# Which pair of heads is masked first, and which engine normalises x: two edits to a four-layer kernel of convolutions and windowed attention

## The chip, the cores and the metric

The kernel runs on one core of one Trainium2 chip. A core has TensorE for matrix products (PE in the profile, its weight loads PEld), VectorE (DVE), ScalarE (ACT) and GpSimd (POOL) for elementwise work, SyncE (SP) that issues transfers, and 16 DMA engines. Each of them works off its own queue of instructions in order, and they wait for each other by semaphores. TensorE writes its results into PSUM[...], from where VectorE and ScalarE read them; GpSimd works on SBUF. The metric is the device time of one execution in microseconds, the median of several runs.

## The reference, cut to what matters

Four layers, each of the form x = x + layer(groupnorm(x)), on x of 4 x 256 x 48 x 48 in float32. Layer 0 builds a 7x7 dilated filter for every pixel from a convolution and a softmax; layers 1 and 2 are 3x3 convolutions with binary and ternary weights. The change is in layer 3, linear attention over boxes of three sizes:

```python
q = sigmoid(einsum('bchw,oc->bohw', x, Wq))      # 8 heads of 32 channels
k = sigmoid(einsum('bchw,oc->bohw', x, Wk))
v = einsum('bchw,oc->bohw', x, Wv);  v = v / max(norm(v, axis=1), 1e-12)
Ik, Ikv = integral(k), integral(einsum('bfhw,bghw->bfghw', k, v))
for w in (1, 2, 4):                              # boxes of 48, 24, 12 pixels
    wk, wkv = box(Ik, 48 // w), box(Ikv, 48 // w)
    attn = einsum('bdhw,bdfhw->bfhw', q, wkv)
    outs.append(attn / (einsum('bdhw,bdhw->bhw', q, wk) + 1e-6))
out = x + einsum('bchw,oc->bohw', concatenate(outs), Wout) + bout
```

Before it, x is group-normalised: (x - m) / sqrt(var + eps), with 32 groups of 8 channels.

## The kernel before, in words

The kernel doesn't form the integrals of k times v. For every block of 8 rows of queries it computes scores k·q against tiles of 8 x 16 keys, multiplies them by 0/1 masks that say which keys lie in the query's box of each of the three sizes, and sums masked scores times v. Layers 0 to 2 run first, image by image, with work of the next image mixed in; the last part is layer 3's attention, over a stream of 720 tiles of scores: 4 images x 2 halves of the channels (4 heads each) x 6 blocks of query rows `rb`, and for each of these the tiles `(a, c)` of keys, `a` the block of 8 rows and `c` one of three columns of 16. A tile is near when its rows fall into the smallest box (`a` at most one block from `rb`: 384 tiles), else far. As far as they last, near and far tiles alternate; what is left follows, mostly near or far alone. The order of all work on each engine is the order of the program.

For a tile `n`, the loop does this:

- `scores` (line 1694 on): TensorE writes `s` for two pairs of heads, first pair, then second. Each pair takes two PSUM banks, and there are two such buffers (`ps_s`), so the first pair of tile n+1 can be written only when the first pair of tile n has been read by all, and so the second.
- `masked` (line 1712): the heart of the change. ScalarE's `copy` takes out the columns where the largest box covers every key of the tile, so that no mask is needed. VectorE's `widest` multiplies the strips beside them by the mask of the largest box, and its `middle` makes the scores of the middle box out of the banks (near tiles only). GpSimd multiplies ScalarE's copy by the mask of the smallest box (near) or the middle one (far). In 192 of the far tiles there is `copy` and `widest`, in the remaining 144 tiles, at the edge of the largest box, only `widest` over the whole tile.
- `sums`: TensorE multiplies the masked scores of tile n-2 by `vs` (LAG = 2), so it has these sums to do between the scores of one tile and those of the next.
- `advance`: one step of the jobs that run beside: the projections to q, k, v of the next image (`Projection`, line 287), box sums of k (`k_sums`), the norms, the final product with `Wout` (`finish`).

`Projection.load` (line 301) fetches 8 rows of x into `xr` and writes them normalised and reordered into `xn`, one instruction for each half of the channels. It takes the mean and the reciprocal deviation from `st3`, which `layer2` fills at its end. It runs for 30 groups of rows, two instructions each: 12 groups for image 0 while layers 0 to 2 of image 3 are still at work, and 6 for each of images 1 to 3, beside the first blocks of the image ahead of it.

The calls whose order is at stake, in `masked`:

```python
first, second = zip(ss, pairs)
copy(*first)
middle(*second)
copy(*second)
middle(*first)
widest(*first)
widest(*second)
```

Every engine's instruction is recorded by one helper, so the profile shows line 142 for almost all; groups are told apart by the names of the tiles: `s` scores, `sm` masked scores, `acc` sums, `proj_ps` projections, `xn` normalised x, `sg`, `kt`, `vt` what ScalarE takes out of the projections.

Of the kernel before, what the change touches and what calls it, by code (L numbers as in the profile page):

```python
# [15 lines left out]
AF = mybir.ActivationFunctionType  # L16
ALU = mybir.AluOpType
# [128 lines left out]
def conv_preact_kernel(  # L146
# [50 lines left out]
    st3 = const.tile([P, B, 2, NCT], F32, name="st3")  # L197


    pe, dve, act, pool, sync = (  # L200
        InOrder(tc, e) for e in (nc.tensor, nc.vector, nc.scalar, nc.gpsimd, nc.sync)
    )
# [69 lines left out]
    def take(what):  # L272
        while free[what] == 0:
            yield 1
        free[what] -= 1
# [11 lines left out]
    class Projection:  # L287
# [13 lines left out]
        def load(self, g, a, n):  # L301

            b = self.b
            yield from take("xr")
            if self.enough:
                free["xr"] += 1
                self.left.append(g)
                return
            xr = self.scr.tile([P, NCT, RB, W], F32, tag="xr", name="xr")
            sync.dma_start(  # L310
                out=xr,
                in_=x3_d[b][:, a * RB : (a + 1) * RB, :].rearrange(
                    "(ct p) r w -> p ct r w", p=P
                ),
            )
            yield FETCH
            yield from take("xn")
            xn = self.scr.tile([P, NCT, NKC, P], F32, tag="xn", name="xn")
            for ct in range(NCT):
                dve.tensor_scalar(  # L320
                    xn[:, ct].rearrange("p c (r x) -> p c r x", x=KC),
                    xr[:, ct].rearrange("p r (c x) -> p c r x", x=KC),
                    st3[:, b, 0, ct : ct + 1],
                    st3[:, b, 1, ct : ct + 1],
                    ALU.subtract,
                    ALU.mult,
                )
                yield 1
            free["xr"] += 1
            self.xn[g], self.uses[g] = xn, n  # L330
# [102 lines left out]
        def groups(self, groups):  # L433

            def load(n):
                a, names = groups[n]
                return self.load(n, a, sum(NKC if name == "v" else 1 for name in names))

            yield load(0)
            for n, (a, names) in enumerate(groups):
                if n + 1 < len(groups):
                    yield load(n + 1)
                for name in names:
                    if name == "v":
                        for c in range(NKC):
                            yield self.v(n, a, c)
                    else:
                        yield self.qk(n, a, name[0], int(name[1]))  # L450


    with (
# [766 lines left out]
        def layer2(b, stats):  # L1220
# [102 lines left out]
            late()  # L1323
            fill(1.5)
            m3, r3 = stats.end(fill)
            dve.tensor_copy(st3[:, b, 0, :], m3)
            dve.tensor_copy(st3[:, b, 1, :], r3)

        def prelude(b):
# [99 lines left out]
        with (  # L1429
# [30 lines left out]
            for b in range(B):  # L1460
                if b + 1 < B:
                    filler = conv0(b + 1, {})
                else:
                    ending.close()
                    wts3 = ctx.enter_context(tc.tile_pool(name="wts_qkv", bufs=1, side="right"))
                    filler = project_first()
                    masks = wts3.tile([P, NMASK], BF16, name="masks")
                    nc.gpsimd.dma_start(out=masks, in_=masks_in[:, 0:NMASK])
                stats = attend(b)
                for _ in side:  # L1470
                    fill(1.5)
                load_wl1(0)
                load_wl1(1)
                load_wl2(0)
                layer2(b, layer1(b, stats))
                if b + 2 < B:
                    prelude(b + 2)
                else:
                    fill_all()
# [3 lines left out]
    with (  # L1483
# [187 lines left out]
        def rows_seen(wi, a, rb):  # L1671

            h = HALVES[wi]
            return (
                max(0, a * RB - h + 1 - rb * RB),
                min(RB, a * RB + RB + h - rb * RB),
            )

        def cols_seen(wi, c):
            h = HALVES[wi]  # L1680
            return max(0, c * KC - h + (wi > 0)), min(W, c * KC + KC + h)

        class Block:
# [28 lines left out]
            def masked(self, a, c, ss):  # L1712

                rb = self.rb
                all0 = rows_seen(0, a, rb), cols_seen(0, c)
                (r0, r1), (c0, c1) = all0
                wis = [wi for wi in range(NW) if seen(wi, a, rb)]
                pairs = [
                    {
                        wi: smp.tile(  # L1720
                            [P, 2, RB, min(W, KC + 2 * HALVES[wi])],
                            F32,
                            tag=f"sm{wi}",
                            name=f"sm{wi}",
                        )
                        for wi in wis
                    }
                    for _ in ss
                ]

                def view(tiles, wi, rows, cols):
                    (y0, _), (x0, _) = rows_seen(wi, a, rb), cols_seen(wi, c)
                    return tiles[wi][
                        :, :, rows[0] - y0 : rows[1] - y0, cols[0] - x0 : cols[1] - x0
                    ]

                def times_mask(engine, wi, rows, cols, dst, src):
                    mr = rb * RB + rows[0] - (a * RB - HALVES[wi] + 1)
                    mc = cols[0] - (c * KC - MCOL0[wi])
                    nr, ncol = rows[1] - rows[0], cols[1] - cols[0]  # L1740
                    m = mask[wi][:, mr : mr + nr, mc : mc + ncol]
                    engine.tensor_mul(
                        dst, src, m.unsqueeze(1).to_broadcast([P, 2, nr, ncol])
                    )

                def of_banks(s, tiles, wi, rows, cols):
                    src = s[:, :, rows[0] - r0 : rows[1] - r0, cols[0] - c0 : cols[1] - c0]
                    times_mask(dve, wi, rows, cols, view(tiles, wi, rows, cols), src)

                f0, f1 = max(0, c * KC + KC - HALVES[0]), min(W, c * KC + HALVES[0] + 1)
                full = abs(a - rb) * RB + RB <= HALVES[0]

                many = seen(NW - 1, a, rb)

                def middle(s, tiles):
                    if full and many:
                        of_banks(s, tiles, 1, rows_seen(1, a, rb), cols_seen(1, c))

                def copy(s, tiles):
                    if full:
                        act.copy(
                            view(tiles, 0, (r0, r1), (f0, f1)), s[:, :, :, f0 - c0 : f1 - c0]
                        )

                def widest(s, tiles):
                    if not full:
                        of_banks(s, tiles, 0, *all0)
                        return  # L1770
                    for p0, p1 in ((c0, f0), (f1, c1)):
                        if p0 < p1:
                            of_banks(s, tiles, 0, (r0, r1), (p0, p1))

                first, second = zip(ss, pairs)
                copy(*first)
                middle(*second)
                copy(*second)  # L1780
                middle(*first)
                widest(*first)
                widest(*second)
                for tiles in pairs:

                    wi = NW - 1 if many else 1
                    if wi in wis:
                        rows, cols = rows_seen(wi, a, rb), cols_seen(wi, c)
                        src = view(tiles, 0, rows, cols)
                        times_mask(pool, wi, rows, cols, view(tiles, wi, rows, cols), src)  # L1790
                return [
                    {wi: view(t, wi, rows_seen(wi, a, rb), cols_seen(wi, c)) for wi in wis}
                    for t in pairs
                ]
# [28 lines left out]
        def seen(wi, a, rb):  # L1823
            r0, r1 = rows_seen(wi, a, rb)
            return r0 < r1
# [226 lines left out]
```

## Time and profile before

| | |
|---|---|
| time, median of 3 runs | 3783.98 us (3771.21 to 3786.39) |
| span of the profiled execution | 3775.4 us |
| TensorE busy, matrix products | 3264.8 us (86%), mean granted clock 0.952 |
| VectorE busy | 2487.2 us (66%), 5119 instructions |
| ScalarE busy | 1036.2 us (27%), 2025 instructions |
| GpSimd busy | 1518.1 us (40%) |
| first scores of layer 3 | 1430 us after the start |
| normalisation of x for q, k, v | 60 instructions on VectorE, 39.2 us |
| masks by VectorE from PSUM | 2592 instructions, 1135.8 us |
| copies by ScalarE from PSUM | 1152 instructions, 594.9 us |

In a row of groups, the columns are line, engine, operation, output and input tiles with their shape, the count; then busy time and the mean of one in ns; then the idle time of the engine just before these instructions, and what ended it. In the timeline, the columns are start, duration, engine, operation, shape and count of the merged instructions, and in brackets the idle time before and its releaser. In the list of waits they are who waited for whom, the total, how often, and the longest, in us. A row of windows gives the stretch, its length, and each engine's busy time with the number of its instructions.

### The profile page before, as it was taken

How to read it: one execution, taken by the hardware profiler on the slowest of the kernel's cores; microseconds unless marked ns; L12 is line 12 of the kernel's file. 1: busy time of each engine (PE TensorE's matmuls, PEld its weight loads, DVE VectorE, ACT ScalarE, POOL GpSimd, SP SyncE). 2: the span in 40 equal slices, each digit the busy share in tenths (PEclk: the TensorE clock that was granted, in tenths of full speed). 3: DMA queues.
4: the chain of work that ended last, by engine and by line, in shares of the span. 5: the costliest groups of instructions: out<-in, count | busy, mean ns of one | idle time of the engine just before them, and what ended most of it. 6: DMA issues, size and time to landing. Idle time of an engine off the chain costs nothing. (4 is left out here: it accounts for less than half of the span.)

```text
span 3775.4 us, 68847 instructions
## 1 busy us (share of the span) xinstructions
PE 3264.8 (86%) x26498; PEld 1879.4 (50%) x26498; DVE 2487.2 (66%) x5119; ACT 1036.2 (27%) x2025; POOL 1518.1 (40%) x2184
## 2 busy tenths in 40 slices
PE   3688898998996788988889889899899899989998
PEld 2467686786784564433334334344443344444443
DVE  7876587587583366777666567756577766556665
ACT  0012111111113322433222333332344332233331
POOL 0000120020020034778765486755365766344332
PEclk9798999999997899999999899999999999999999
DMA  7745323324324313345434243533223444101122
GB/s 250 238 135 170 100 104 116 109 95 125 109 75 124 102 70 108 125 136 159 125 103 131 90 136 122 164 97 108 78 95 123 139 116 116 47 31 53 41 60 60
DMA packets 373019, 423.04 MB, mean 112 GB/s; under 512 B 129076, under 2 KB 328532, under 8 KB 371540
## 3 DMA queue, kind: packets, MB, share of 16 engines
q1 hardware_dynamic: 371491, 416.32, 35.6%
q8 instruction: 211, 3.46, 0.4%
q0 software_dynamic: 144, 1.52, 0.2%
q14 instruction: 117, 0.95, 0.1%
q10 hardware_dynamic: 1056, 0.79, 0.1%
HBM read 288.79 MB, written 131.25 MB: 111 GB/s over the span
## 5 line engine op out<-in xcount | busy, mean ns | idle before, releaser
L142 DVE TENSOR_TENSOR sm<-s,masks 128x112 f32<-128x112 f32 (+10 forms) x2592 | 1135.8, 493 | 765.5 <-PE s L142 321.1
L142 POOL TENSOR_TENSOR sm<-sm,masks 128x432 f32<-128x432 f32 (+14 forms) x1152 | 853.3, 755 | 936.5 <-ACT sm L142 672.0
L142 PE MATMUL s<-qs,ks 32*128 32x320 f32 (+3 forms) x5760 | 832.5, 500 | 200.1 <-DVE sm L142 151.2
L142 ACT COPY sm<-s 128x528 f32<-128x528 f32 (+2 forms) x1152 | 594.9, 535 | 1470.7 <-PE s L142 1169.9
L142 PE MATMUL acc<-sm,vs 128*32 128x384 f32 (+18 forms) x13440 | 880.5, 385 | 16.1 <-POOL sm L142 15.8
L142 PEld LDWEIGHTS s<-qs,ks 32*128 32x128 f32 x5760 | 374.1, 185 | 604.7 <-DVE sm L142 232.8
L142 PE MATMUL cv<-vx,wt 128*128 128x288 f32 x2080 | 559.3, 425 | 90.7 <-DVE vx L142 49.1
L142 PEld LDWEIGHTS acc<-sm,vs 128*32 128x32 f32 x13440 | 355.2, 110 | 551.3 <-issue 348.6
L142 PEld LDWEIGHTS cv<-vx,wt 128*128 128x128 f32 x2080 | 402.4, 198 | 212.4 <-issue 53.6
L142 POOL MEMSET v<- 128x16 f32 (+1 forms) x120 | 18.6, 215 | 725.7 <-DVE vx L142 635.7
L142 PE MATMUL cv<-v,wl 128*128 128x384 f32 x1152 | 224.5, 354 | 24.4 <-DVE x L142 9.2
L142 PEld LDWEIGHTS cv<-v,wl 128*128 128x128 f32 x1152 | 214.8, 195 | 34.6 <-issue 16.1
L142 POOL TENSOR_TENSOR pt<-pt 128x144 f32<-128x144 f32 x336 | 187.4, 558 | 22.8 <-DVE pt L142 0.5
L142 POOL TENSOR_TENSOR v<-l2v,v 128x384 fp32r<-128x384 f32 x96 | 109.2, 1168 | 130.2 <-ACT v L142 121.4
L142 POOL TENSOR_TENSOR nhi<-nhi,nq 128x384 f32<-128x384 f32 x144 | 148.3, 1058 | 0.0
L142 PE MATMUL cv<-pad,wl 128*128 128x384 bf16 x864 | 143.1, 327 | 0.0
L142 PE MATMUL out_ps<-o,wout_sb 128*128 128x384 f32 x288 | 122.8, 509 | 9.4 <-DVE o L142 5.4
L142 PE MATMUL out_ps<-stage,wout_sb 128*128 128x384 f32 x288 | 117.3, 489 | 0.4 <-DVE stage L142 0.4
L142 PE MATMUL proj_ps<-wv_sb,xn 128*128 128x256 f32 x288 | 89.5, 438 | 32.3 <-ACT vt L142 19.1
L142 DVE TENSOR_TENSOR vx<-v 128x868 f32<-128x868 f32 x112 | 115.4, 1056 | 0.5
L142 PE MATMUL ap<-seen,xT 120*128 120x120 f32 (+3 forms) x832 | 113.5, 293 | 0.0
L142 PEld LDWEIGHTS <-wl 128*128 128x128 bf16 x864 | 83.8, 97 | 59.1 <-issue 0.4
(162 smaller groups left out, 2859.0 us busy)
## 6 DMA issues: line engine op xcount, KB each, us to landing
wt<-wt SPq DMA_DIRECT2D x48, 768.0 KB
kb_d<-pt SPq DMA_DIRECT2D x48, 576.0 KB
rc<-r_d SPq DMA_DIRECT2D x192, 144.0 KB
nhi<-kb_d SPq DMA_DIRECT2D x120, 192.0 KB
nlo<-kb_d SPq DMA_DIRECT2D x88, 192.0 KB
o_d<-stage SPq DMA_DIRECT2D x24, 576.0 KB
o<-o_d SPq DMA_DIRECT2D x24, 576.0 KB
wl<-wl_d SPq DMA_DIRECT2D x16, 768.0 KB
```

The source lines that it names most:

```text
L142: return lambda *args, **kwargs: self.tc.keep_in_program_order(op(*args, **kwargs))
```

## The change

Two edits in layer 3. In `masked`, VectorE's `middle` now takes the first pair of heads ahead of the second, after both copies have been issued. In `Projection.load`, the rows of x are normalised by ScalarE in one activation, scale * x + bias, in place of VectorE's (x - m) * r; for this `layer2` stores -m * r in place of m.

```diff
@@ Projection.load
             for ct in range(NCT):
-                dve.tensor_scalar(
+                act.activation(
                     xn[:, ct].rearrange("p c (r x) -> p c r x", x=KC),
                     xr[:, ct].rearrange("p r (c x) -> p c r x", x=KC),
-                    st3[:, b, 0, ct : ct + 1],
-                    st3[:, b, 1, ct : ct + 1],
-                    ALU.subtract,
-                    ALU.mult,
+                    AF.Identity,
+                    bias=st3[:, b, 0, ct : ct + 1],
+                    scale=st3[:, b, 1, ct : ct + 1],
                 )
                 yield 1
@@ layer2
             m3, r3 = stats.end(fill)
-            dve.tensor_copy(st3[:, b, 0, :], m3)
+            dve.scalar_tensor_tensor(st3[:, b, 0, :], m3, -1.0, r3, ALU.mult, ALU.mult)
             dve.tensor_copy(st3[:, b, 1, :], r3)
@@ masked
                 first, second = zip(ss, pairs)
                 copy(*first)
-                middle(*second)
                 copy(*second)
                 middle(*first)
+                middle(*second)
                 widest(*first)
                 widest(*second)
```

## The prediction

> **What bounds the kernel now.** I read the busy times first, then stretches of the run, then the waits of the stretch that the change is in, then its groups of instructions by shape, and last the order in time of two tiles of scores. The chain of waits explains only a few per cent of this span, so I don't use it. The stretches before and after the first scores:
>
> ```profile
> core 0: us, PE busy (x) PEld busy (x) DVE busy (x) ACT busy (x) POOL busy (x), PEclk, DMA share, GB/s
> 0.00:1431.00 1431.00, 1184.39 (x5842) 936.56 (x5842) 940.38 (x1831) 262.55 (x489) 153.90 (x298) 0.92 0.40 128
> 1431.00:3775.00 2344.00, 2080.36 (x20660) 942.85 (x20656) 1546.86 (x3288) 773.64 (x1536) 1364.18 (x1886) 0.97 0.34 103
> ```
>
> Layer 3's attention is the second row: 2344 us, of which TensorE (PE) is busy 2080 and idle 264. VectorE (DVE) is busy 66% of it, ScalarE (ACT) 33%. The waits there, what TensorE waits for first:
>
> ```profile
> PE s L142 <- DVE sm L142: 151.2, 243, 3.9
> PE proj_ps L142 <- ACT sg L142: 18.3, 14, 6.1
> PE acc L142 <- POOL sm L142: 15.8, 17, 3.3
> ...
> DVE sm L142 <- PE s L142: 321.1, 342, 9.2
> DVE sm L142 <- ACT sm L142: 266.9, 181, 5.5
> ```
>
> More than half of TensorE's idle time (151 of 264 us) is one wait: new scores (`s`) can't be written until VectorE has masked the old ones out of the same banks. And VectorE waits 321 us for scores. The two wait for each other in turn: a loop, in which nothing is hidden whenever TensorE has no sums left to do. The shapes that matter:
>
> ```profile
> L142 ACT COPY sm<-s 128x528 f32<-128x528 f32 x384 | 229.1, 615 | 489.0 <-PE s L142 382.4 <-DVE sm L142 79.6 <-POOL sm L142 21.6
> L142 DVE TENSOR_TENSOR sm<-s,masks 128x624 f32<-128x624 f32 x256 | 194.9, 802 | 98.3 <-PE s L142 94.2 <-ACT sm L142 3.2 <-POOL sm L142 0.8
> L142 DVE TENSOR_SCALAR xn<-xr,st 128x384 f32<-128x384 f32 x60 | 39.2, 665 | 31.4 <-PE proj_ps L142 27.3 <-DMA xr<-x_d 4.1
> ```
>
> The first row is `copy`, the second `middle` for tiles of the middle columns, the third the normalisation that moves. `copy` waits 79.6 us for VectorE: that is the second pair's copy waiting until `middle` of the second pair has read the same scores. One tile in time, its loop closed on TensorE:
>
> ```profile
> 3028.46 1.19 PE L142 MATMUL s<-qs,ks 32*128 32x320 f32 x8 [0.83 <-DVE sm L142]
> 3029.36 0.51 ACT L142 COPY sm<-s 128x400 f32<-128x400 f32 x1 [1.43 <-PE s L142]
> 3029.68 1.78 DVE L142 TENSOR_TENSOR sm<-s,masks 128x448 f32<-128x448 f32 x4 [0.99 <-PE s L142]
> 3030.40 0.51 ACT L142 COPY sm<-s 128x400 f32<-128x400 f32 x1 [0.53 <-DVE sm L142]
> 3031.30 1.03 PE L142 MATMUL s<-qs,ks 32*128 32x320 f32 x8 [1.04 <-DVE sm L142]
> ```
>
> ScalarE starts on the first pair at 3029.36, VectorE on the second pair at 3029.68, only 0.32 us later; at 3030.40 ScalarE turns to the second pair. They never read one pair together.
>
> **What the Trainium skill says.** "PSUM — Partial Sum Buffer", section "PSUM bank collisions raise a hardware error": two engines may not touch one bank and quadrant at once, two readers included, and the compiler's scheduler puts a dependency between them. The trace agrees: over all 384 tiles with a `middle`, where VectorE waited for a copy it started 32 ns after the copy's end, and the second copy began 34 to 90 ns after `middle` of its pair. The same page, "Engine vs sequencer instructions", calls the queues of ScalarE and VectorE strict FIFO: what waits holds up what is behind it. "ScalarE: Activation LUTs", "Table sets: the hidden batching unit", puts cheap functions such as identity into every set, so the new activation needs no load of its own; the changed program indeed has 68 loads, like the one before (`ACT_TABLE_LOAD` x68, 1283 ns each).
>
> **The change, part by part.**
>
> *Order of the pairs.* Nothing is added or removed. Before, VectorE's first `middle` took the second pair and waited only for TensorE, while ScalarE copied the first pair. Now it takes the first pair, which ScalarE is copying (`copy(*first)` still stands ahead), so it must wait for that copy: the instruction's wait changes from TensorE to ScalarE. Queued behind it on VectorE are `middle` of the second pair, the border strips of both pairs, and with them TensorE's next scores. In the tile shown, the copy ends at 3029.36 + 0.51 = 3029.87; VectorE can start 0.03 later, at 3029.90, instead of 3029.68: 0.22 us late. After that its four instructions follow one another as before (the second copy then overlaps `middle` of the first pair: 0.51 against 0.62 us, so no second wait), the border of the first pair ends 0.22 later, and TensorE, which started its next scores 0.10 us after that border, starts 0.22 later too.
>
> I did the same sum for each of the 384 tiles with a `middle`: end of the first copy + 0.03, or where VectorE was still busy then, its actual start, less the actual start of `middle`. The lateness is 0.17 us in the mean and 78 us in all, counting tiles where it is positive. From each I took off TensorE's slack there: the time from the release of the scores to TensorE's next scores, beyond the shortest delays (0.10 us for the first pair, 0.14 for the second). In 209 tiles there is less than 0.1 us of slack; their lateness comes to 45 us. In the others TensorE still has sums, norms or projections to do, and the delay is hidden by these: summing each tile's excess over its slack, 44 us remain on the path. By columns: 26 us from the 128 tiles of the middle columns (copy of 615 ns), 7 and 11 us from the two edge columns (480 and 509 ns). A tile's delay moves all that follows by the same amount, so I add them: **+44 us**.
>
> In return the second pair's copy no longer waits for VectorE and ends up to half a microsecond earlier. GpSimd masks from that copy, but of 215 waits of TensorE for GpSimd's masked scores, one follows such a second copy directly: worth under 1 us. ScalarE's work behind that copy (`sg`, `vt`, `ns`, `stage`) comes earlier as well; TensorE waits for it some 50 us in the stretch, mostly in long single waits for a table load or a transfer, and I take a tenth: **-5 us**.
>
> *Normalisation on ScalarE.* 60 `tensor_scalar` of 665 ns leave VectorE (39.2 us). 24 of them stand before 1431 us, 36 in the attention. In the attention I went through the 36: in 12 of them VectorE had no idle time between the normalisation and the next mask, and TensorE took up the scores at once; there about 0.6 us each is gained: **-7 us**. The other 24 stood in VectorE's idle time. On ScalarE 60 activations are added. The trace has no such activation of 128x384. From below, `sg` with one scale and no pointers took 496 ns; by the price of "ScalarE: Activation LUTs", "What ACT_TABLE_LOAD costs" (186 ns, 0.833 ns an element, 93 ns for each pointer), 692 ns; from above, the activation of 128x1152 with both pointers took 1472 ns against 1332 by that price, so up to 0.83. I take 0.7: 42 us in all, 25 in the attention, where ScalarE is idle 1570 us. Its waits: the transfer of `xr`, issued four steps earlier (one wait, 4.1 us, in the run before), and TensorE's last matmul on the old `xn`. Queued behind it is the next first copy, on which VectorE now hangs. But the next scores stand behind that matmul on TensorE and take some 0.6 us until they can be copied, so of 0.7 about 0.1 shows, for half of the 36: **+2 us**.
>
> *Normalisation before 1431 us.* 24 instructions move in the stretch where image 0 is projected beside layers 0 to 2 of image 3. VectorE loses six waits for TensorE (27.3 us); ScalarE takes them over, behind copies of `vt` that themselves wait for transfers (22.8 us). TensorE waited 15 us for `xn`. It will wait for it on the other engine. **0**, by at most 5 either way.
>
> *Shift in the statistics.* One copy of 164 ns becomes one operation on 128x2, of about 160 ns as its neighbours: four in all, **0**.
>
> Sum: 44 - 5 - 7 + 2 = **+34 us**, 3784 + 34 = 3818 us.
>
> **The rivals.** (a) *Hidden*: TensorE is busy 89% of the attention and absorbs the delays; then what is left is the relief of VectorE and ScalarE, -12 + 2, with a third of the delay (15): about 3789 us. For it: 175 of 384 tiles have slack today. Against: slack was already taken off, and 151 us of waiting for VectorE sit exactly in this loop. Chance 0.17. (b) *Faster*: all 39 us of normalisation were on VectorE's path and the first pair gets masked sooner because it is scored sooner; 3784 - 39 = 3745 us. For it: VectorE is in the loop. Against: it has 800 us of idle time there, and the first pair isn't free sooner, ScalarE holds it. Chance 0.09. (c) *Slower by more*: every delay shows, 78 us, since slack used up once isn't there for the next delay: 3862 us. Part of the slowest fifth of the main case.
>
> **How the numbers follow.** The main case, slower by 20 to 75 us, has 0.74. Half a per cent is 19 us, so slower 0.74, same 0.17, faster 0.09. The range runs from a little under no change (3778; it leaves out (b)) to 3856 (it leaves out the far end of (c)).
>
> **What would show it.** In the trace after: the first `middle` of a tile waits for the copy, so VectorE's waits for `s` on TensorE shrink from 321 us and those on ScalarE's `sm` grow well above 267; ScalarE's 235 us of waits for VectorE's `sm` fall to almost nothing; TensorE's 151 us for VectorE rise by some 40; the stretch from the first scores grows from 2344 to about 2378 us and the 1431 before it stay within 5; `xn` on ScalarE measures 0.65 to 0.83 us. I'm wrong if TensorE's wait for VectorE doesn't grow, or if the first stretch changes by more than 10 us.

## The result, and the profile after

The changed kernel takes 3838.43 us (median of 4 runs, 3835.74 to 3840.08) against 3785.18 us of the kernel before on the same chip (3771.21 to 3788.22): ratio 1.0147, 95% interval 1.0121 to 1.0173. It is slower by 53 us.

Stretches before and after the first scores (columns as before: the stretch, its length, busy time of each engine, the granted clock, which is the share of full speed at which TensorE was let run, and transfers):

```profile
0.00:1425.00 1425.00, 1175.75 (x5838) 931.46 (x5842) 924.70 (x1800) 276.73 (x513) 153.52 (x298) 0.92 0.40 128
1425.00:3838.00 2413.00, 2115.14 (x20664) 967.19 (x20663) 1515.95 (x3259) 775.95 (x1573) 1343.78 (x1886) 0.96 0.34 100
```

All the loss is in the attention: from the first scores to the end it took 2346 us before and takes 2413 now. The first stretch ends 5 us earlier, but so it does in a run below in which nothing of it was changed, so this is taken for scatter. The two traces lie 63 us apart, a little more than the medians of the runs. In the attention TensorE is busy 35 us longer, with the same instructions, and idle 34 us longer (2413 - 2115 = 298, from 264). VectorE is busy 31 us less (24 of it the normalisations that left) and has gained nothing by it. Who waits for whom there:

```profile
PE s L142 <- DVE sm L142: 197.1, 271, 5.2
PE s L142 <- issue: 22.4, 24, 1.4
PE proj_ps L142 <- ACT sg L142: 14.1, 12, 4.7
PE acc L142 <- POOL sm L142: 13.8, 14, 4.2
...
DVE sm L142 <- ACT sm L142: 638.6, 545, 10.3
...
DVE sm L142 <- PE s L142: 52.7, 29, 5.5
```

VectorE's masks now wait for ScalarE (639 us, from 267) where they waited for TensorE (53, from 321). TensorE's waits before new scores rise by 54 us: 197.1 for VectorE, 22.4 without a releaser that the profile shows (`issue`) and 0.2 for ScalarE's `sm`, together 219.7; before they were 151.2, 0.6 and 13.7, together 165.5. The groups:

```profile
L142 ACT COPY sm<-s 128x528 f32<-128x528 f32 x384 | 219.8, 616 | 487.0 <-PE s L142 343.8 <-POOL sm L142 74.2 <-issue 48.8
L142 DVE TENSOR_TENSOR sm<-s,masks 128x624 f32<-128x624 f32 x256 | 195.2, 803 | 139.9 <-ACT sm L142 139.2 <-issue 0.6
L142 ACT ACTIVATE xn<-xr,st 128x384 f32<-128x384 f32 x60 | 41.2, 708 | 14.5 <-PE proj_ps L142 12.9 <-DMA xr<-x_d 1.6
```

No instruction of the masks became slower (616 against 615 ns, 803 against 802); the idle time ahead of `middle` grew from 98 to 140 us and changed its cause. The copy no longer waits for VectorE. The same tile as in the prediction, in time:

```profile
3069.31 1.19 PE L142 MATMUL s<-qs,ks 32*128 32x320 f32 x8 [0.83 <-DVE sm L142]
3070.20 0.91 ACT L142 COPY sm<-s 128x400 f32<-128x400 f32 x2 [2.32 <-PE s L142]
3070.74 1.78 DVE L142 TENSOR_TENSOR sm<-s,masks 128x448 f32<-128x448 f32 x4 [1.20 <-ACT sm L142]
3072.36 0.54 PE L142 MATMUL s<-qs,ks 32*128 32x320 f32 x2 [1.25 <-DVE sm L142]
```

ScalarE copies both pairs without a pause, VectorE starts 1.43 us after the scores began (1.22 before), and the next scores follow after 3.05 us (2.84 before): 0.21 us later, in a tile for which the prediction worked out 0.22.

TensorE's extra busy time has its own cause. Five stretches of 3.4 us of the changed kernel, a little earlier:

```profile
3022.70:3026.10 3.40, 2.14 (x33) 0.97 (x32) 3.23 (x9) 2.24 (x5) 3.17 (x5) 1.00 0.00 0
3026.10:3029.50 3.40, 1.90 (x16) 0.81 (x16) 2.43 (x9) 1.16 (x3) 2.77 (x4) 0.99 0.68 251
3029.50:3032.90 3.40, 3.30 (x18) 1.52 (x22) 2.44 (x6) 1.34 (x3) 2.79 (x4) 0.50 0.18 54
3032.90:3036.30 3.40, 3.40 (x32) 1.16 (x24) 1.31 (x3) 0.00 (x0) 2.57 (x5) 0.50 0.06 11
3036.30:3039.70 3.40, 3.29 (x48) 1.50 (x44) 1.95 (x5) 1.78 (x4) 1.86 (x4) 1.00 0.00 0
```

The first number after the length is TensorE's busy time, the first after the engines its granted clock. In two stretches running it was busy for 2.14 and 1.90 of 3.4 us; in the two that follow it runs at half speed, though now there is work with hardly a gap (3.30 and 3.40 us busy). Adding up the clock records of the attention, half speed covers 127 us before and 184 after. One kernel's figure scatters by some 20 us from trace to trace (140 and 120 for the same kernel in e5_swap_xn and e10_swap_xn below), so the rise is clear and its size is not exact.

### The profile page after: what moved, and what is told of

It is laid out like the page before. It is cut to its first block, busy times and chain, and to the rows that moved or that the text cites. A ratio compares the mean times of both kernels' runs of the same rounds, so it can differ in the third digit from the quotient of the medians.

```text
span 3838.0 us, 68765 instructions
## 1 busy us (share of the span) xinstructions
PE 3290.9 (86%) x26498; PEld 1898.7 (49%) x26498; DVE 2440.6 (64%) x5059; ACT 1052.7 (27%) x2085; POOL 1497.3 (39%) x2184
## 5 line engine op out<-in xcount | busy, mean ns | idle before, releaser
L142 PE MATMUL s<-qs,ks 32*128 32x320 f32 (+3 forms) x5760 | 854.2, 506 | 243.4 <-DVE sm L142 197.1
L142 ACT COPY sm<-s 128x528 f32<-128x528 f32 (+2 forms) x1152 | 572.8, 535 | 1513.6 <-PE s L142 1218.7
L142 PEld LDWEIGHTS s<-qs,ks 32*128 32x128 f32 x5760 | 393.8, 188 | 648.2 <-issue 291.4
L142 DVE SCALAR_TENSOR_TENSOR x<-cv,alpha,x 128x384 f32<-128x384 f32 x144 | 83.9, 610 | 45.7 <-PE cv L142 45.3
```

The lines of the kernel that those rows point to most:

```text
L142: return lambda *args, **kwargs: self.tc.keep_in_program_order(op(*args, **kwargs))
```

## The experiments

All times are against the kernel before, in runs on the same chip. "Late" is how much later than before the border strips of the first pair end, counted from the start of the tile's scores, averaged over the three columns of keys: 3.05 us before. For e4_swap and e5_swap_xn it is left out, since there the copy of the first pair, and no longer its strips, ends last.

| kernel | median, us | ratio (95%) | late, us | half speed, us |
|---|---|---|---|---|
| changed kernel | 3838.43 | 1.0147 (1.0121 to 1.0173) | +0.20 | 184 |
| e1_order | 3836.37 | 1.0139 (1.0121 to 1.0157) | +0.20 | 197 |
| e2_xn | 3779.04 | 0.9997 (0.9982 to 1.0011) | 0.00 | 142 |
| e3_mirror | 3804.21 | 1.0063 (1.0050 to 1.0077) | +0.07 | 156 |
| e4_swap | 3740.80 | 0.9891 (0.9879 to 0.9904) | | 118 |
| e5_swap_xn | 3738.83 | 0.9870 (0.9849 to 0.9891) | | 140 |
| e6_copy2_before | 3857.26 | 1.0183 (1.0162 to 1.0204) | +0.21 | 207 |
| e7_copy2_order | 4051.66 | 1.0698 (1.0676 to 1.0720) | +0.78 | 371 |
| e8_warm | 3845.75 | 1.0151 (1.0127 to 1.0175) | +0.19 | 149 |

**The two parts apart: e1_order and e2_xn.** e1_order is the kernel before with

```diff
 copy(*first)
-middle(*second)
 copy(*second)
 middle(*first)
+middle(*second)
 widest(*first)
```

and e2_xn is the changed kernel with this taken back.

> The order of the pairs alone, with the normalisation still on VectorE. If the wait for ScalarE's copy is the cause: +45 to +65 us on the kernel before (3830 to 3850), VectorE's waits for ScalarE's sm near 640 us and for TensorE's s near 50 us, the stretch before the first scores unchanged. If the normalisation on ScalarE is what costs (by holding up the first copies): within 15 us of the kernel before.

> The normalisation on ScalarE alone, second pair masked first as before. If the prediction's count holds: 5 to 10 us under the kernel before (about 3777), of it up to 5 us before the first scores. If the normalisation costs by holding up copies: 10 to 30 us over it.

The order alone costs 54 us (1.0139), as much as the whole change. Its waits in the attention, VectorE's and ScalarE's roles turned as expected:

```profile
PE s L142 <- DVE sm L142: 193.2, 268, 3.5
PE s L142 <- issue: 24.2, 24, 1.4
...
DVE sm L142 <- ACT sm L142: 627.2, 528, 10.3
...
DVE sm L142 <- PE s L142: 56.6, 30, 4.8
```

The normalisation alone changes nothing that can be told from scatter: 0.9997, from 7 us faster to 4 us slower. Neither its gain of 5 to 10 us is confirmed, nor any loss.

**The same order of pairs without the wait: e3_mirror.** In near tiles, on the kernel before:

```diff
-copy(*first)
-middle(*second)
-copy(*second)
-middle(*first)
+middle(*first)
+copy(*second)
+middle(*second)
+copy(*first)
 widest(*first)
 widest(*second)
```

> In near tiles VectorE takes the first pair first, as in the changed kernel, but ScalarE copies the second pair first, so that neither finds the other on its pair. If the wait for the copy is the cause: within 15 us of the kernel before (VectorE starts some 0.4 us earlier on the first pair and gives most of it back waiting for the second pair's copy). If masking the first pair ahead of the second costs by itself: 40 to 60 us slower, as the changed kernel is.

It lost 24 us by the ratio (22 by the medians), less than half of the changed kernel's loss, and outside both expectations. The trace shows a smaller wait of the same kind: VectorE starts on the first pair 0.3 us earlier than it started before, but `middle` of the second pair must wait for the second copy, which ends 1.85 to 2.09 us after the start of the scores, and starts 0.02 to 0.07 us later than the second of the two `middle`s did before (0.00 in the middle column). The strips end 0.07 us late. So this run alone doesn't part the order from the wait; that the first pair going first costs nothing by itself is shown by e4_swap below, which masks it first too and is faster than the kernel before.

**How the loss grows with the wait: e6_copy2_before and e7_copy2_order.** In near tiles the first copy is made twice, in the order of before and in the changed one:

```diff
 copy(*first)
+if many:
+    copy(*first)
```

> The order of before, with the first pair's copy of every near tile made twice (the same values again), so that ScalarE holds the first pair some 0.45 to 0.55 us longer. VectorE takes the second pair meanwhile and reaches the first 0.5 to 0.53 us after the end of a single copy; if the order of before hides the copy, the second one just fits: within 20 us of the kernel before. If ScalarE's time by itself counts (384 copies, some 190 us of work): 60 us slower or more.

> The same doubled copy in the changed order (normalisation on VectorE). If VectorE's first mask hangs on the end of that copy, every near tile's masks start 0.45 to 0.55 us later than with the changed order alone, and some 220 to 280 of 384 show it: 100 to 150 us over the changed order alone, 150 to 210 over the kernel before. If the changed order costs for another reason: about the same step from the order alone as the doubled copy makes on the kernel before.

Both were slower than expected. A part of it is that two copies don't overlap: the second begins 0.03 us after the first has ended, so the first pair is held 0.51 to 0.65 us longer, where 0.45 to 0.55 was expected. In the order of before that runs past the moment at which VectorE comes for the first pair (2.14 instead of 1.94 us in the first column): strips 0.21 us late, 69 us lost. This is the lateness of the changed order with the order of before, and a loss of the same size. By the time alone it also fits the other reading, that ScalarE's time counts by itself (60 us or more). The waits speak against that. TensorE's for VectorE's masks, in e6_copy2_before and then in e7_copy2_order, are

```profile
PE s L142 <- DVE sm L142: 220.5, 280, 3.9
PE s L142 <- DVE sm L142: 351.1, 327, 4.9
```

against 151.2 before, so in e6_copy2_before they rose by 69 us, while its waits for ScalarE's other work (`sg`, `ns`, `vt`, `stage`) fell from 53 to 43 us. In the changed order the strips are 0.78 us late, and 264 us are lost. So the doubled copy costs 69 us in one order and some 210 in the other, and over four kernels the loss follows the lateness: 24 us at 0.07, 54 at 0.20, 69 at 0.21, 264 at 0.78, or 270 to 340 us for each us. Not all of this is waiting: in e7 TensorE's idle time in the attention grew by 172 us (264 to 436), and 244 us more at half speed make up to 122.

**The clock: e8_warm.** The changed order with

```diff
+if n < len(stream) and 0 < at and not last and stream[n][2] > 0 and seen(...):
+    for _ in range(2):
+        pe.matmul(blocks[i].accs[0], zeros[:, 0:P], zeros, start=False, stop=False)
```

> The changed order, with two products of zeros (128x384, added to an open sum, so that no value changes) after the sums of near tiles of the second and third column of keys, where TensorE mostly waits for masks. If half-speed stretches of TensorE's clock, which follow its idle time, are a part of the loss: half-speed time in the attention back from 183 us to 130 or less, and up to 25 us under the changed order alone, less what the products cost where TensorE isn't waiting (about 0.3 us in some 70 tiles, 20 us). If the clock plays no part: 20 to 60 us over the changed order alone.

The attention of e1_order, as stretches of the run:

```profile
1425.00:3840.00 2415.00, 2117.84 (x20664) 968.64 (x20660) 1531.61 (x3295) 754.60 (x1536) 1343.26 (x1886) 0.96 0.33 100
```

and of e8_warm:

```profile
1425.00:3848.00 2423.00, 2194.30 (x21182) 992.90 (x21181) 1537.33 (x3305) 754.79 (x1537) 1344.29 (x1886) 0.97 0.33 100
```

518 matmuls more make TensorE busy 76 us longer, and the kernel is no faster and no slower than with the order alone (1.0151 against 1.0139, intervals overlapping). Half speed went from 197 us to 149 (from 183 to 135 without the stretch that runs across the first scores), not quite to the 130 that were expected. Most of the added work filled idle time (297 to 226 us). This agrees with the clock being a part of the loss, about 24 us for the 48 us less of half speed, but the added work and the filled gaps are as large, so the run alone doesn't prove it.

**A better order: e4_swap, e5_swap_xn, and GpSimd's order.** If the release of scores sets the pace, VectorE should finish the first pair before it turns to the second. In near tiles:

```diff
-copy(*first)
-middle(*second)
-copy(*second)
 middle(*first)
+widest(*first)
+copy(*second)
+copy(*first)
+middle(*second)
-widest(*first)
 widest(*second)
```

e4_swap is the kernel before with this edit; e5_swap_xn is the changed kernel with its calls put in the same order.

> In near tiles VectorE does all it has on the first pair (middle, then the border strips) while ScalarE copies the second, then they change places. If the release of the first pair's scores sets TensorE's next start: the first pair free 0.4 us earlier in the tile, some 200 tiles of it on the path, -30 to -60 us on the kernel before. If TensorE is the limit there, or the later copy of the first pair holds up GpSimd: within 15 us of it.

> The exchange of pairs of e4 with the normalisation on ScalarE, both parts of the change kept and only the order of copies and strips different. If the normalisation is worth nothing: 3735 to 3745 us, as e4. If ScalarE, which now copies both pairs late in a tile, is held up by it: 5 to 20 us over e4. If VectorE's relief counts now that it is ahead: 5 to 10 us under e4.

41 us are gained (0.9891). The same tile of e4_swap:

```profile
3023.65 1.51 PE L142 MATMUL s<-qs,ks 32*128 32x320 f32 x8
3024.50 0.94 DVE L142 TENSOR_TENSOR sm<-s,masks 128x448 f32<-128x448 f32 x2 [0.30 <-PE s L142]
3025.27 0.91 ACT L142 COPY sm<-s 128x400 f32<-128x400 f32 x2 [1.67 <-PE s L142]
3025.81 0.94 DVE L142 TENSOR_TENSOR sm<-s,masks 128x448 f32<-128x448 f32 x2 [0.37 <-ACT sm L142]
3026.23 1.47 PE L142 MATMUL s<-qs,ks 32*128 32x320 f32 x8 [0.46 <-ACT sm L142]
```

VectorE does the first pair in one go (0.94 us), then the second; ScalarE the other way round. The next scores start 2.58 us after these, for 2.84 before and 3.05 in the changed kernel, and now it is ScalarE's copy that TensorE waits for. Over the attention, TensorE's waits for masks before new scores fell from 165 us to 118:

```profile
PE s L142 <- ACT sm L142: 66.3, 115, 3.4
PE s L142 <- DVE sm L142: 51.9, 98, 4.5
```

With the normalisation on ScalarE (e5_swap_xn) the ratio is 0.9870, not to be told from e4_swap.

In that order the copy of the second pair is ready first, so in e9_swap_pool GpSimd masks it first:

```diff
-for tiles in pairs:
+for tiles in (pairs[::-1] if many else pairs):
```

> e5 (exchange of pairs, normalisation on ScalarE), and GpSimd masks the second pair of near tiles ahead of the first, since in this order ScalarE's copy of the second pair ends 0.65 us before that of the first. If GpSimd's late masks hold TensorE's sums (22 us of such waits in e4): 5 to 15 us under e5, 3725 to 3735. If the masks are in time anyway, being needed two tiles later: as e5, within 5 us.

It took 3726.32 us, 0.9851 (0.9828 to 0.9875), which the interval doesn't part from e5_swap_xn, run on another chip. So the two ran again side by side, and a third with VectorE's normalisation:

> The kernel of e5 once more, beside the next two on one chip: 0.985 to 0.989 of the kernel before.

> The kernel of e9 once more. If GpSimd's order of the pairs is worth something: 5 to 15 us under e10. If not: within 5 us of it.

> As e11, with the normalisation back on VectorE. If ScalarE's normalisation helps in this order of work: 5 to 10 us over e11. If it is worth nothing, as in the order of before: within 5 us of e11.

e10_swap_xn took 3736.82 us (0.9888, 0.9871 to 0.9906), e11_swap_pool 3721.24 (0.9847, 0.9832 to 0.9862), e12_swap_pool_dve 3731.56 (0.9876, 0.9857 to 0.9894). GpSimd's order is worth some 15 us: the intervals are apart. The 10 us by which ScalarE's normalisation is ahead in this order are not sure, as the intervals overlap a little. Why GpSimd's order helps was not followed further: TensorE's direct waits for GpSimd's masks hardly changed (20.8 us in e5, 20.2 in e9). e11_swap_pool, the fastest, is 58 us faster than the kernel before on its chip; against that kernel the changed one stands at 1.0147 and this one at 0.9847.

## Why the prediction was right, and where its sizes were off

*The order of the pairs.* The mechanism held at each step: the wait changed from TensorE to ScalarE, `middle` started late, the strips and the release of the scores with it, and e3, e6 and e7 show the loss to follow that lateness in either order. The lateness was forecast at 0.17 us and measured at 0.20. The term of +44 us was too small: the order alone cost 54. In the traces of the kernel before and the changed one, whose attention differs by 67 us, the pieces are these. TensorE's waits before new scores grew by 54 us (forecast 44), so its slack hid some 23 of the 77 us of lateness (0.20 us in 384 tiles), where 34 of 78 had been taken off. Its waits for ScalarE's work other than `sm` fell by 16 us, from 53 to 37 (forecast -5). That this is work which is no longer held up isn't shown: in e6_copy2_before and e7_copy2_order, where ScalarE has more to do, these waits fell too, to 43 and 38 us. And TensorE ran at half speed 57 us longer, which at half the work per us is up to 28 us. That last piece was missing from the sum. It was in part offset by the fall in the waits for ScalarE, put at 5 us instead of 16, and it is partly luck that the misses didn't add up. The Trainium skill, "TensorE: Matmul & The Clock Gate", "Part 1: The HAM clock gate (the "warmup" mystery)", says that the clock falls to half after an idle window of about 3.4 us; the prediction didn't reckon that longer gaps bring more such windows. The trace agrees in the length and in the half; but here the clock fell after windows that were only some 40% idle (2.14 and 1.90 us busy of 3.4, with one gap of 2.5 us across both), where that section speaks of an idle one.

By columns the forecast was less good than in sum: the tiles of the first column of keys became longer by 23 us in all (forecast 7), those of the middle one by 28 (26), of the last by 6.5 (11); the 7 us belong to the first column, with copies of 509 ns, and the 11 to the last, with 480, though the prediction names the two durations the other way round. Why the first column lost so much where it had slack wasn't settled; half-speed stretches that begin in its tiles last 44 us against 17 before, but in e1_order, where this column also lost 23 us, they last 27, so the clock isn't the account.

*Normalisation.* An activation took 708 ns; 0.7 us was taken, between 496 ns of a simpler one and an upper figure of 0.83, and close to the estimate of 692 ns from the price in the Trainium skill, "ScalarE: Activation LUTs", "What ACT_TABLE_LOAD costs", with which the trace thus agrees. Its net worth in the attention, -7 + 2 us, and the 0 ahead of it, lie inside what e2_xn measured (-7 to +4), which can't tell them from nothing.

*The rivals.* Hidden by TensorE (a) fell: it left 15 us of the delay, and the waits before new scores grew by 54. Faster (b) fell: VectorE lost 39 us of work and stood idle instead. Of (c), that every delay shows, more is true than the prediction gave it. If each tile's delay showed, a kernel would lose 384 us for each us of lateness; measured are 270 to 340, seven to nine tenths of that. In waiting alone it is less: in e7_copy2_order, with 0.78 us of lateness in 384 tiles (300 us), TensorE's idle time grew by 172 us, so a good part stays hidden there, and up to 122 us of the loss go with the clock. The changed kernel's 53 us remain clear of the 78 that (c) forecast.

## What to carry to other kernels

Where two engines take turns on the same buffers, look at what the first instruction of each waits for: an order in which the second engine starts on the buffer that the first is still reading turns a free start into a wait, and everything behind it in its queue is late. Sum the lateness tile by tile, less the slack of the engine that is fed; and where the gaps of TensorE get longer, allow for its clock: here up to 28 us of the loss. To gain in such a loop, let each engine finish what it has on one buffer before it changes to the other, since the release of the first buffer sets the next start: that, and not taking work off an engine that is idle a third of the time, was worth 41 us here.

## What the runs showed of the hardware that was not expected

TensorE's granted clock fell to 0.50 for stretches of 3.4 us or multiples of it, and no long pause was needed. If the attention of all fourteen traces is cut into windows of 3.4 us along the edges of these stretches, the windows at full speed in which TensorE was busy (by the profile's count) for less than 40% of the time were all followed by half speed (151 of 151), those at 70% or more never (0 of 8119), and those between in 252 of 787 cases. In the changed kernel the window before a stretch was up to 69% busy, and in 16 of 35 cases the one before that was busy 90% or more, so a single window of broken work was enough. The half-speed time of the attention ran from 118 us in e4_swap to 371 us in e7_copy2_order.

Two copies by ScalarE of the same 128x384 to 128x528 values to the same place didn't overlap at all: the second began 0.03 us after the first one's end. Copies of two different pairs do overlap: in the changed kernel's tile above, two of 0.51 us took 0.91 together.
